# First two token tiles centred and turned through a diagonal of factors, head 0's q and k in alternating halves, head 4's q projected one slot earlier, in a four-block transformer kernel

## The chip, the cores and the metric

The kernel runs on one core of a Trainium2 chip. The time is the device time of one execution in microseconds. Three runs of the kernel before gave 628.95, 629.01 and 629.42 us, a median of 629.01 us. Engines are named as the profile names them: PE is the matrix engine (PEld its weight loads), DVE the vector engine, ACT the scalar engine, POOL the general-purpose engine, SP the engine that issues most DMAs.

## The reference, cut to what matters

Input `h` has 2 batches of 512 tokens and 256 features. Four blocks follow one another, each with a residual and layer norms around it; the change lies in the first block alone, softmax attention with 16 heads of 128:

```python
x = L0_attn_h
x = x + _layernorm(_L0_attn_ref(_layernorm(x), ...))          # 16 heads, softmax, rotary
x = x + _layernorm(_L0_ffn_ref(_layernorm(x), ...))           # 4-bit weights, gelu
x = x + _layernorm(_L1_attn_ref(_layernorm(x), ...))          # linear attention
x = x + _layernorm(_L1_ffn_ref(_layernorm(x), ...))           # looked-up weights, silu

def _L0_attn_ref(h, wq, bq, ...):
    x = (h - mu) * rsqrt(var + EPS) * ln_g + ln_b
    q = rope((x @ wq.T + bq).reshape(b, s, 16, 128))
    k = rope((x @ wk.T + bk).reshape(b, s, 16, 128))
    v = (x @ wv.T + bv).reshape(b, s, 16, 128)
    attn = softmax(where(causal, -inf, q k^T / sqrt(128)))
    return (attn @ v) @ wo.T + bo + h
```

The first block's input is normalised twice in a row (once outside, once inside), which the kernel folds into one factor per token.

## The kernel before, in words

Tokens are worked in tiles of 128 (`NT` = 4 tiles to a batch). All arithmetic is float32. Instructions are issued in the order in which the Python code runs, and each engine works through its own instructions in that order; across engines a tile's readers and writers wait for one another. Tiles come from pools of one or two buffers, and a buffer is written again when its last reader is done.

**The start.** `first_norms(0, 0.0)` (lines 554 to 688) normalises batch 0. For each tile DVE takes `statistics` (line 600) and `variance` (603); `factor` (606) adds the epsilons on DVE (`ve`) and raises to -0.5 on POOL (`rstd`). For tiles 0 and 1, `finished(t, pool)` (593) lets POOL form `shift = -mean * rstd` and ACT write `n = rstd * x + shift`. Tiles 2 and 3 are written by DVE in `centred` (609). PE transposes the eight 128x128 pieces of `n` (`turn`, 620) into two banks `halves`, ACT applies gain and bias (`affine`, 623) and so writes `xT0`, features on partitions and tokens along the free axis, in four pieces of 256 tokens. POOL and ACT copy it in another order to `xTv`. Before all that PE multiplies the identity by itself `WARM` = 9 times (line 538), and once more between tile 0 and tile 1 (line 662).

**The projections.** `projection(kind, i, tag)` (786) makes q or k of head `i` (heads of both batches are numbered 0 to 31): two matmuls, then the rotary turn. `a = (ps + bias) * cos` is one pass over 128x512, done by DVE, or by ACT with a POOL product behind it; `r` is two DVE passes over 64 partitions (`rr`), with `sin`; `a + r` is `qT` or `kT`. Head 0's q is done in two halves of 256 tokens, every other projection in one piece. `values` (826) makes v of two heads. Weights of two heads come in one load (`load`, 509) into one of two buffers per kind.

**The slots.** After q 0, k 0, the first v and q 1 (lines 1100 to 1103), `slot(i)` (998) runs once per head. In it PE does, in this order: scores of head `i` (6 matmul records in bank s, 2 in bank t), q of head `i+1`, k of head `i+1`, `projected_out(i-2)`, `attended(i-1)` (894), one `values`. q of head 3 is the exception: it is issued in slot 1 through the generator `ahead` (line 1078) ahead of `attended(0)`, and slot 2 leaves q out.

**The turned softmax.** `turned_p(i)` (876) has DVE transpose blocks of p into `turned` (one buffer), then SP issues four DMAs that bring it to `pT[i]`, a tile of a pool with one buffer (line 885). So the DMAs of head `i` start when `attended(i-1)`, the reader of the buffer, has ended; and the DVE transposes of head `i+1` wait until those DMAs have read `turned`.

Of the kernel before, what the change touches and what calls it, by code (L numbers as in the profile page):

```python
# [38 lines left out]
EPS = 1e-5  # L39
EPS_LIN = 1e-9  # L40
NEG = -1e30
WARM = 9
REST = INTER - (NO - 1) * P


# [143 lines left out]
def sandwich_kernel(  # L189
# [309 lines left out]
    with ExitStack() as at:  # L499
# [54 lines left out]
        def first_norms(b, wait):  # L554

            n = [
                acts.tile([P, HT, D], F32, tag="ln", name=f"n0_{b}_{j}") for j in range(NT // HT)  # L560
            ]
            st = small.tile([P, NT, 6], F32, tag="st0", name="st0", bufs=2)
            mv = small.tile([P, NT, 2], F32, tag="mv0", name="mv0", bufs=2)
            ve = small.tile([P, 2, NT], F32, tag="ve0", name="ve0", bufs=2)
            rstd = small.tile([P, 2, NT], F32, tag="rstd0", name="rstd0", bufs=2)
            shift = small.tile([P, 2, NT], F32, tag="shift0", name="shift0", bufs=2)

            def factors(k, ts, scale, more):
                vector.tensor_scalar(
                    ve[:, k, ts], mv[:, ts, 1], scale, more, ALU.mult, ALU.add  # L570
                )
                pool.tensor_tensor(rstd[:, k, ts], ve[:, k, ts], mhalf[:, ts], ALU.pow)

            def shifted(k, ts):
                vector.scalar_tensor_tensor(
                    shift[:, k, ts], mv[:, ts, 0], -1.0, rstd[:, k, ts], ALU.mult, ALU.mult
                )

            def shifted_row(t):
                pool.tensor_scalar(  # L580
                    shift[:, 0, t : t + 1], mv[:, t, 0:1], rstd[:, 0, t : t + 1], -1.0, ALU.mult, ALU.mult
                )

            def norm(k, t, to):
                scalar.activation(
                    to,
                    x0[b][:, t, :],
                    AF.Identity,
                    bias=shift[:, k, t : t + 1],
                    scale=rstd[:, k, t : t + 1],  # L590
                )

            def finished(t, engine=vector):
                if engine is pool:
                    shifted_row(t)
                else:
                    shifted(0, slice(t, t + 1))
                norm(0, t, n[t // HT][:, t % HT, :])

            def statistics(t):  # L600
                vector.bn_stats(st[:, t, :], x0[b][:, t, :])

            def variance(t):
                vector.bn_aggr(mv[:, t, :], st[:, t, :])

            def factor(t):
                factors(0, slice(t, t + 1), 1.0 + EPS, EPS * EPS)

            def centred(t):

                vector.tensor_scalar(
                    n[t // HT][:, t % HT, :],
                    x0[b][:, t, :],
                    mv[:, t, 0:1],
                    rstd[:, 0, t : t + 1],
                    ALU.subtract,
                    ALU.mult,
                )

            def turn(pt, kc, t):  # L620
                transpose(pt, n[t // HT][:, t % HT, kc * P : (kc + 1) * P])

            def affine(engine, to, pt, kc):
                if engine is scalar:
                    scalar.activation(to, pt, AF.Identity, bias=col("b", kc), scale=col("g", kc))
                else:
                    vector.tensor_scalar(to, pt, col("g", kc), col("b", kc), ALU.mult, ALU.add)

            if wait:
                for t in range(NT):  # L630
                    statistics(t)
                    variance(t)
                    factor(t)
                    if t:
                        finished(t - 1)
                    yield wait
                finished(NT - 1)
                yield 2 * wait
                for kc in range(NK):
                    pt = bank("t")  # L640
                    for t in range(NT):
                        turn(pt[:, t * P : (t + 1) * P], kc, t)
                    affine(scalar, xT0[b][:, kc, :], pt, kc)
                    yield wait
            else:


                for t in range(NT):
                    statistics(t)
                    variance(t)  # L650
                    factor(t)
                    if t < HT:
                        finished(t, pool)
                centred(2)
                centred(3)
                halves = [bank("t") for _ in range(2)]
                for t in range(NT):
                    for kc in range(NK):
                        at = kc * TU + t % 2 * P
                        turn(halves[t // 2][:, at : at + P], kc, t)  # L660
                    if t == 0:
                        warm_up(1)
                for j in range(2):
                    for kc in range(NK):
                        affine(
                            scalar,
                            xT0[b][:, kc, j * TU : (j + 1) * TU],
                            halves[j][:, kc * TU : (kc + 1) * TU],
                            kc,
                        )  # L670
            for kc in range(NK):
                (scalar.copy if kc or wait else pool.tensor_copy)(
                    xTv[b][:, kc, :].rearrange("p (t a j) -> p t j a", t=NT, j=4),
                    xT0[b][:, kc, :].rearrange("p (t j a) -> p t j a", t=NT, j=4),
                )
            yield 30.0
            while holder[0] is not None:
                yield 4.0
            holder[0] = b
            every = slice(0, NT)  # L680
            factors(1, every, 1.0, EPS)
            yield 2.0
            shifted(1, every)
            yield 2.0
            for t in range(NT):
                norm(1, t, acc[:, t, :])
                pool.tensor_add(acc[:, t, :], acc[:, t, :], bo_sb)
                yield 3.0

        first = first_norms(0, 0.0)  # L690
        begin(first, next(first))
        pool.affine_select(
            out=mask,
            in_=mask,
            compare_op=ALU.is_ge,
            fill=NEG,
            base=S - P,
            pattern=[[-1, S]],
            channel_multiplier=1,
        )  # L700

        def dequantised(packed, scales, u, name, w):

# [82 lines left out]
        def projection(kind, i, tag="mm"):  # L786
# [7 lines left out]
            to = qk.tile([P, S], F32, tag=f"T{kind}", name=f"{kind}T")  # L794
            lo, hi = slice(0, 64), slice(64, 128)

            for cs in [slice(0, TU), slice(TU, S)] if (kind, i) == ("q", 0) else [slice(0, S)]:
                ps = bank(tag)
                for kc in range(NK):
                    matmul(  # L800
                        ps[:, cs],
                        w[:, kc, hh * DK : (hh + 1) * DK],
                        xT0[b][:, kc, cs],
                        kc == 0,
                        kc == NK - 1,
                    )
                yield
                if (kind == "k") == (i > 1) and i:
                    scalar.activation(a, ps, AF.Identity, bias=bias)
                    pool.tensor_mul(a, a, cos_sb)  # L810
                else:
                    vector.scalar_tensor_tensor(
                        a[:, cs], ps[:, cs], bias, cos_sb[:, cs], ALU.add, ALU.mult
                    )
                vector.scalar_tensor_tensor(
                    r[lo, cs], ps[hi, cs], bias[hi], sin_sb[hi, cs], ALU.add, ALU.mult
                )
                vector.scalar_tensor_tensor(
                    r[hi, cs], ps[lo, cs], bias[lo], sin_sb[lo, cs], ALU.add, ALU.mult
                )  # L820
            if (kind, i) == ("k", 1):
                inverted(0)
            (pool if i > 1 or kind == "q" else vector).tensor_add(to, a, r)
# [174 lines left out]
        def slot(i):  # L998
            b, h = divmod(i, NH)
            g2, odd = divmod(i, HG)  # L1000
            if i == 2:
                load("q", 2)
                load("k", 2)
            if odd == 0:
                load("v", g2 + 2)
# [45 lines left out]
            else:  # L1051
                assert not terms
            for kind in "qk":
                if (kind, i) in (("q", 0), ("q", 2)):
                    pass
                elif i + 1 < NS:
                    project(kind, i + 1)
# [15 lines left out]
                values(0, 1, "t")  # L1073
            elif i == 1:
                values(1, 1, "t")
            if i == 1:

                ahead = projection("q", 3)
                next(ahead)
            if 1 <= i < NS + 1:  # L1080
                attended(i - 1)
# [1 line left out]
                values(1, 0)  # L1083
            if now_in:
                turned_p(i)
            if i == 1:
                next(ahead, None)
            poll()
            if i < NS - HG:
# [7 lines left out]
                look_up(done)  # L1097
            catch_up()

        project("q", 0)  # L1100
        project("k", 0, "o")
        values(0, 0, "t")
        project("q", 1, "o")

# [310 lines left out]
```

## Time and profile before

| | |
|---|---|
| median of three runs | 629.01 us |
| the profiled execution's own time | 629.14 us |
| span of its profile | 627.3 us |
| PE's first matmul on data (a transpose) | 5.66 us |
| first `xT` piece begun by ACT | 7.01 us |
| first score matmul of head 0 | 14.99 us |
| first score matmul of head 1 | 22.39 us |
| last matmul's end in the chain of waits | 619.76 us |
| granted clock of PE in every slice | 0.9 or more of full |

A line of a timeline gives start, duration (both in us), engine, line of the code, operation, what it writes and reads, its shape, how many records are merged, and in brackets the idle time of the engine before it with what ended it. A float32 matmul leaves two records. A group of PE records ends later than the next group starts[...]; so I compare starts with starts. Line 181 and line 163 are those of a helper that records each instruction, so instructions are told apart by the tiles they write and read.

### The profile page before, as it was taken

To read this page: it belongs to the slowest core of one execution; us is meant where nothing else is said; L and a number is where in the kernel's file an instruction comes from. 1 tells how busy PE (TensorE), PEld (TensorE's weight loads), DVE (VectorE), ACT (ScalarE), POOL (GpSimd) and SP (SyncE) were. 2 spreads that over 40 slices of the span, in tenths; PEclk is the share of its full clock that TensorE was granted. 3 is DMA by queue.
4 is the path that set the end of the run, shared out by engine and by line. 5 is a ranking of instruction groups with operands and counts; after the bars stand their busy time and mean duration, and the time that the engine had idled before them with its cause. 6 is when DMAs were issued, how large, how long until landed. Compare 5 with 4: busy or idle time off the path is not lost.

```text
span 627.3 us, 8200 instructions
## 1 busy us (share of the span) xinstructions
PE 619.3 (99%) x2504; PEld 461.7 (74%) x2504; DVE 486.5 (78%) x1154; ACT 298.1 (48%) x654; POOL 276.8 (44%) x350
## 2 busy tenths in 40 slices
PE   8999999999999999999999999999999999999996
PEld 6656666666666666666666778888888888888886
DVE  6969889878877989999988988769986373284853
ACT  4655666666655566656656661232313404416130
POOL 4354657446355375575667400350261151163341
PEclk9999999999999999999999999999999999999999
DMA  7376475464565656557453322211001001001000
GB/s 252 89 182 178 118 179 153 107 192 121 130 169 137 151 151 156 152 135 184 125 133 82 85 54 67 101 35 34 1 2 33 1 1 35 0 2 33 26 27 17
DMA packets 42428, 60.07 MB, mean 96 GB/s; under 512 B 5008, under 2 KB 29840, under 8 KB 42384
## 3 DMA queue, kind: packets, MB, share of 16 engines
q1 hardware_dynamic: 42096, 59.39, 36.3%
q8 instruction: 20, 0.33, 0.2%
q14 instruction: 24, 0.20, 0.1%
q10 hardware_dynamic: 288, 0.16, 0.1%
HBM read 28.33 MB, written 1.05 MB: 47 GB/s over the span
## 4 chain that ended last, share of the span: by engine, by line
PE 96%; DMA 1%; POOL 1%; issue 0%; DVE 0%; SPq 0%; POOLq 0%
PE ps_mm L272 39%; PE ps_o L272 22%; PE ps_s L272 21%; PE ps_t L272 14%; DMA pT<-turned 1%; POOL rstd L181 0%; DMA x<-in_x 0%; SPq L163 0%; PE ps_t L278 0%; DVE st L181 0%; POOL shift L181 0%; POOLq L1411 0%; DVE x L181 0%; DVE n L181 0%; DVE mv L181 0%
## 5 line engine op out<-in xcount | busy, mean ns | idle before, releaser
L181 POOL TENSOR_TENSOR wg<-wg,scratch 128x752 f32<-128x752 f32 x30 | 53.7, 1791 | 95.1 <-DVE scratch L181 95.1
L181 DVE SCALAR_TENSOR_TENSOR rr<-ps_mm,cols_sb,sin_sb 64x512 f32<-64x512 f32 (+1 forms) x126 | 93.4, 741 | 2.8 <-ACT ra L181 0.4
L272 PE MATMUL ps_mm<-xT,wg 128*128 128x256 f32 (+1 forms) x352 | 84.9, 379 | 0.0
L181 ACT ACTIVATE p<-p,mn 128x512 f32<-128x512 f32 (+3 forms) x128 | 70.6, 552 | 29.3 <-DVE mn L181 29.3
L272 PE MATMUL ps_s<-xT,wu 128*128 128x256 f32 x336 | 81.0, 379 | 0.0
L272 PE MATMUL ps_o<-wd,hT 128*128 128x256 f32 (+1 forms) x364 | 78.2, 372 | 0.0
L272 PE MATMUL ps_t<-pT,v 128*128 128x512 f32 (+3 forms) x256 | 74.3, 433 | 1.3 <-DMA pT<-turned 1.3
L272 PEld LDWEIGHTS ps_o<-wd,hT 128*128 128x128 f32 x364 | 67.4, 190 | 8.8
L272 PEld LDWEIGHTS ps_mm<-xT,wg 128*128 128x128 f32 (+1 forms) x352 | 66.4, 189 | 9.3 <-ACT ge L181 0.3
L272 PEld LDWEIGHTS ps_s<-xT,wu 128*128 128x128 f32 x336 | 63.8, 190 | 8.7
L272 PEld LDWEIGHTS ps_t<-pT,v 128*128 128x128 f32 x256 | 48.6, 190 | 29.2 <-issue 17.5
L181 DVE CUSTOM_DVE_ANT_0 p<-ps_s,mask 128x512 f32<-128x512 f32 (+2 forms) x96 | 45.9, 509 | 30.3 <-PE ps_s L272 30.1
L181 ACT ACTIVATE p<-p,rs 128x512 f32<-128x512 f32 (+3 forms) x128 | 61.4, 550 | 10.8 <-DVE rs L181 8.8
L272 PEld LDWEIGHTS ps_o<-wo,oT 128*128 128x128 f32 x256 | 48.6, 190 | 19.0 <-issue 13.2
L181 POOL TENSOR_TENSOR qT<-ra,rr 128x512 f32<-128x512 f32 x32 | 40.9, 1277 | 48.0 <-DVE rr L181 46.2
L272 PE MATMUL ps_s<-kT,qT 128*128 128x512 f32 (+2 forms) x192 | 60.8, 452 | 0.1
L272 PE MATMUL ps_o<-wo,oT 128*128 128x256 f32 x256 | 60.5, 379 | 0.0
L272 PE MATMUL ps_mm<-xT,wq 128*128 128x512 f32 (+1 forms) x128 | 58.4, 580 | 0.0
L272 PE MATMUL ps_mm<-xT,wk 128*128 128x512 f32 x124 | 58.3, 592 | 0.0
L181 DVE STREAM_TRANSPOSE turned<-p 128x512 f32<-128x512 f32 (+3 forms) x128 | 54.1, 480 | 2.1 <-DMA pT<-turned 1.0
L272 PEld LDWEIGHTS ps_s<-kT,qT 128*128 128x128 f32 x192 | 36.0, 190 | 26.8 <-issue 15.9
L272 PE MATMUL ps_mm<-wv,xTv 128*128 128x256 f32 x232 | 54.9, 379 | 0.0
(138 smaller groups left out, 910.6 us busy)
## 6 DMA issues: line engine op xcount, KB each, us to landing
pT<-turned SPq DMA_DIRECT2D x128, 208.0 KB, 3.8
wo<-in_wo SPq DMA_DIRECT2D x17, 256.0 KB, 4.2
wq<-in_wq SPq DMA_DIRECT2D x16, 256.0 KB, 4.0
wk<-in_wk SPq DMA_DIRECT2D x16, 256.0 KB, 4.1
wv<-in_wv SPq DMA_DIRECT2D x16, 256.0 KB, 4.1
xT<-tr SPq DMA_DIRECT2D x44, 64.0 KB, 2.1
pk_g<-in_gate_p SPq DMA_DIRECT2D x4, 256.0 KB, 4.9
sc_g<-in_gate_s SPq DMA_DIRECT2D x8, 128.0 KB, 4.6
```

The costliest lines, as they stand in the source:

```text
L181: return write(*args, **more)
L272: nc.tensor.matmul(out, lhsT=lhsT, rhs=rhs, start=start, stop=stop, **more)
```

## The change

Tiles 0 and 1: ACT writes `mean - x` as soon as the mean is known, without the factor. `rstd` of both tiles comes from one pair of two-element instructions. ACT builds, per tile, a diagonal matrix with `-rstd` (from `minus`, the negated identity; all three lie in the tile `wu`, which is not yet in use). Four ordinary matmuls with that diagonal as the moving operand then turn and scale `n` at once. Tiles 2 and 3 are still transposed with the identity; their four transposes stand after q 0's first half, since `first_norms` now yields in between.

Head 0: q and k both come in halves, in the order q first half, (transposes of tiles 2 and 3), k first half, q second half, k second half. In the first halves DVE does the two `rr` passes first, and the `a` pass goes to ACT and POOL (`by_scalar`). POOL's `affine_select` of the mask moves from before head 0 to behind it.

Head 4: its q is issued in slot 2 through `ahead`, in front of `attended(1)`; slot 3 leaves q out. Its weights (`load("q", 2)`) are loaded in slot 0 in place of slot 2. `WARM` goes from 9 to 10, and the single warm-up matmul between tiles goes.

```diff
-WARM = 9
+WARM = 10
...
-            def factor(t):
-                factors(0, slice(t, t + 1), 1.0 + EPS, EPS * EPS)
+            def factor(t, n=1):
+                factors(0, slice(t, t + n), 1.0 + EPS, EPS * EPS)
...
+                minus = wu[:, 0, :P]
+                scalar.mul(minus, ident, -1.0)
                 for t in range(NT):
                     statistics(t)
                     variance(t)
-                    factor(t)
                     if t < HT:
-                        finished(t, pool)
+                        scalar.activation(
+                            n[0][:, t, :], x0[b][:, t, :], AF.Identity, bias=mv[:, t, 0:1], scale=-1.0
+                        )
+                    if t % HT:
+                        factor(t - 1, HT)
+                halves = [bank("t") for _ in range(2)]
+                for t in range(HT):
+                    scalar.activation(
+                        wu[:, 0, (t + 1) * P : (t + 2) * P],
+                        minus,
+                        AF.Identity,
+                        scale=rstd[:, 0, t : t + 1],
+                    )
+                for kc in range(NK):
+                    for t in range(HT):
+                        matmul(
+                            halves[0][:, kc * TU + t * P : kc * TU + (t + 1) * P],
+                            n[0][:, t, kc * P : (kc + 1) * P],
+                            wu[:, 0, (t + 1) * P : (t + 2) * P],
+                            True,
+                            True,
+                        )
                 centred(2)
                 centred(3)
-                halves = [bank("t") for _ in range(2)]
-                for t in range(NT):
-                    for kc in range(NK):
-                        at = kc * TU + t % 2 * P
-                        turn(halves[t // 2][:, at : at + P], kc, t)
-                    if t == 0:
-                        warm_up(1)
                 for j in range(2):
+                    if j:
+                        yield 0.0
+                        for kc in range(NK):
+                            for t in (HT, HT + 1):
+                                at = kc * TU + t % 2 * P
+                                turn(halves[1][:, at : at + P], kc, t)
...
-            for cs in [slice(0, TU), slice(TU, S)] if (kind, i) == ("q", 0) else [slice(0, S)]:
+            for cs in [slice(0, TU), slice(TU, S)] if i == 0 else [slice(0, S)]:
...
-                if (kind == "k") == (i > 1) and i:
-                    scalar.activation(a, ps, AF.Identity, bias=bias)
-                    pool.tensor_mul(a, a, cos_sb)
-                else:
+                def by_scalar():
+                    scalar.activation(a[:, cs], ps[:, cs], AF.Identity, bias=bias)
+                    pool.tensor_mul(a[:, cs], a[:, cs], cos_sb[:, cs])
+
+
+                first_half = i == 0 and cs.start == 0
+                if i and (kind == "k") == (i > 1):
+                    by_scalar()
+                elif not first_half:
...
+                if first_half:
+                    by_scalar()
...
-            if i == 2:
+            if i == 0:
                 load("q", 2)
+            elif i == 2:
                 load("k", 2)
...
-                if (kind, i) in (("q", 0), ("q", 2)):
+                if kind == "q" and i in (0, 2, 3):
...
-            if i == 1:
-
-                ahead = projection("q", 3)
+            if i in (1, 2):
+
+                ahead = projection("q", i + 2)
                 next(ahead)
...
-            if i == 1:
+            if i in (1, 2):
                 next(ahead, None)
...
-        project("q", 0)
-        project("k", 0, "o")
+        pair = projection("q", 0), projection("k", 0, "o")
+        next(pair[0])
+        begin(first, next(first))
+        next(pair[1])
+        for step in (*pair, *pair):
+            next(step, None)
+        pool.affine_select(
...
         values(0, 0, "t")
         project("q", 1, "o")
```

More of the change, by code (lines that the diff above doesn't have):

```diff
@@ L577, in shifted @@
                 )
[L579 to L582, printed above, removed]
             def norm(k, t, to):
@@ L591, in norm, with finished @@
                 )
-            def finished(t, engine=vector):
-                if engine is pool:
-                    shifted_row(t)
-                else:
-                    shifted(0, slice(t, t + 1))
+            def finished(t):
+                shifted(0, slice(t, t + 1))
                 norm(0, t, n[t // HT][:, t % HT, :])
@@ L690, in sandwich_kernel @@
         first = first_norms(0, 0.0)
[L691 to L700, printed above, removed]
+        next(first)
         def dequantised(packed, scales, u, name, w):
@@ L807, in projection @@
                 yield
-                if (kind == "k") == (i > 1) and i:
-                    scalar.activation(a, ps, AF.Identity, bias=bias)
-                    pool.tensor_mul(a, a, cos_sb)
-                else:
+                def by_scalar():
[5 more added lines that the diff above has]
+                elif not first_half:
                     vector.scalar_tensor_tensor(
@@ L1098, in slot @@
             catch_up()
-        project("q", 0)
-        project("k", 0, "o")
+        pair = projection("q", 0), projection("k", 0, "o")
[5 more added lines that the diff above has]
+        pool.affine_select(
+            out=mask,
+            in_=mask,
+            compare_op=ALU.is_ge,
+            fill=NEG,
+            base=S - P,
+            pattern=[[-1, S]],
+            channel_multiplier=1,
+        )
         values(0, 0, "t")
```

## The prediction, made before the changed kernel ran

> **What bounds the kernel.** I read the page first: which engine is full, and what still ends its idle time. Then PE's timeline around the one wait that the page names, then the chain of waits across it, then the timeline of the start.
>
> ```profile
> span 627.3 us, 8200 instructions
> ...
> PE 619.3 (99%) x2504; PEld 461.7 (74%) x2504; DVE 486.5 (78%) x1154; ACT 298.1 (48%) x654; POOL 276.8 (44%) x350
> ...
> L272 PE MATMUL ps_t<-pT,v 128*128 128x512 f32 (+3 forms) x256 | 74.3, 433 | 1.3 <-DMA pT<-turned 1.3
> ```
>
> PE is busy 619.3 of 627.3 us. So an edit pays only if it shortens PE's work, or one of the few stretches in which PE stands: the start, one wait of 1.3 us on the DMA that brings pT, and the tail after the last matmul (619.76 us), which the change does not touch. PE's timeline shows the wait:
>
> ```profile
> 37.49 1.89 PE L272 MATMUL ps_o<-wo,oT 128*128 128x256 f32 x8
> 40.73 2.39 PE L272 MATMUL ps_t<-pT,v 128*128 128x512 f32 x8 [1.34 <-DMA pT<-turned]
> 42.96 1.89 PE L272 MATMUL ps_mm<-wv,xTv 128*128 128x256 f32 x8
> ...
> 52.00 2.32 PE L272 MATMUL ps_t<-pT,v 128*128 128x512 f32 x8
> 54.16 1.89 PE L272 MATMUL ps_mm<-wv,xTv 128*128 128x256 f32 x8
> ```
>
> An eight-record group starts 1.72 us after the one before it (50.28 to 52.00 in slot 3), so `attended(1)` could have started at 37.49 + 1.72 = 39.21; it started at 40.73, 1.52 late, and then took 2.23 (to 42.96) where slot 3's takes 2.16. The wait costs 1.52 + 0.07 = **1.6 us**. The chain of waits says why:
>
> ```profile
> 31.62 2.17 PE ps_t L272 x8
> 33.79 0.02 issue
> 33.81 0.54 SPq L163
> ...
> 35.95 4.64 DMA pT<-turned
> 40.59 0.14 issue
> 40.73 2.39 PE ps_t L272 x8
> ```
>
> pT has one buffer, so head 1's DMAs go out only when `attended(0)` has ended (33.79); issue and landing take to 40.59, and 0.14 later PE goes on: 40.73 - 33.79 = 6.94 us of turnaround. PE has too little to put in between: scores 2.16, k 1.72, out 1.72, in all 5.6.
>
> The start, as the timeline has it:
>
> ```profile
> 3.60 0.18 DVE L181 BATCH_NORM_AGGREGATE mv<-st 128x2 f32<-128x6 f32 x1
> 4.05 0.55 POOL L181 TENSOR_TENSOR rstd<-ve,mhalf 128x1 f32<-128x1 f32 x1 [2.25 <-DVE ve L181]
> 6.03 0.39 PE L536 MATMUL ps_o<-ident 128*128 128x128 f32 x2
> 6.54 1.28 PE L278 MATMUL ps_t<-ident,n 128*128 128x128 f32 x6
> 7.01 1.93 ACT L181 ACTIVATE xT<-ps_t,cols_sb 128x256 f32<-128x256 f32 x4 [0.53 <-PE ps_t L278]
> 7.65 2.05 PE L272 MATMUL ps_mm<-xT,wq 128*128 128x256 f32 x8
> 12.98 1.88 PE L272 MATMUL ps_o<-xT,wq 128*128 128x512 f32 x4
> 14.15 0.69 DVE L181 TENSOR_TENSOR kT<-ra,rr 128x512 f32<-128x512 f32 x1
> 14.99 1.96 PE L272 MATMUL ps_s<-kT,qT 128*128 128x512 f32 x6
> ```
>
> From 7.65 on PE is full, but for a short stall before the scores: q 1 starts at 12.98, so PE was free at 14.70; DVE's kT was done at 14.84 and the scores began at 14.99.
>
> **Part 1: q of head 4 into slot 2.** 1.72 us of PE work moves in front of `attended(1)`: 5.6 + 1.72 = 7.32 us against a turnaround of 6.94. The wait goes with 0.38 to spare: **-1.6 us**. What is late next is slot 3, which loses those 1.72. Between the end of `attended(1)` and `attended(2)` there are values 1.73, scores 2.16, k 1.72, out 1.72, again 7.33. Head 2's DMAs in the trace of before: `attended(1)` ends at 43.12 (40.73 + 2.39), the fourth is issued at 45.4 and lands after 4.3, 49.7, and with the same 0.14 PE could start 6.72 after the end. 0.6 to spare, cost nothing; slot 4's four needed 57.2 + 5.0 = 62.2, which is 7.9 after 54.32 (52.00 + 2.32), and such a landing in slot 3 would cost 8.0 - 7.33 = 0.7. I take the row of the same head, and keep 0.7.
>
> The other instructions of the moved step: DVE's `ra` and two `rr` (0.75 + 1.51 = 2.26) fall behind head 2's block transposes, which end at 42.41; DVE sits idle from there for 3.29 us until 45.75, so they are hidden, and slot 3's DVE is the freer by as much. POOL's qT sum (1.27) stands ahead of the four-element rstd of batch 0's second norm, which nothing waits for in that slot. In slot 3 POOL does the look-up sum (49.40 to 51.18, 6.5 after the slot's first score at 44.69), then k 4's product and sum, 2 x 1.27: kT at about 9.1 after that score, and the next scores come at 2.16 + 1.72 + 1.72 + 2.16 + 1.73 = 9.5. 0.2 to 0.4 to spare.
>
> The load of head 4's wq moves in SP's queue from slot 2 to slot 0, ahead of wv, wo and head 0's pT. It waits for q 1, the last reader of its buffer (about 15 us); wv behind it goes out at 20.86 because it waits for v's own readers, so nothing is held up. From 16 to 20 us the page's DMA row is near nothing, so it lands free. In slot 2 the loads behind head 1's pT are one fewer.
>
> **Part 2: the diagonal.** Removed: four POOL instructions for tiles 0 and 1 (two rstd, two shift) in series; added: one rstd of two elements, two diagonals, and matmuls for transposes. DVE: without the `ve` in between, tile 1's statistics start about 0.10 after 3.60, at 3.70 (before 3.88). Its aggregate is 0.45 later and `ve` 0.22 after that: 4.37. POOL starts 0.24 after `ve` as in the row: 4.61. One element takes 0.55, four take 1.03 (42.53 us), so two about 0.71: 5.32. ACT starts 0.04 later. Its two `mean - x` passes (0.60 each) and the negated identity are then done: they end by about 5.1. The diagonals: a 128x128 product by a column takes ACT 0.387, the second starts about 0.29 behind: ready at 5.75 and 6.04. PE follows 0.06 later; its second matmul starts at 6.10, two more at a spacing of 0.21, and the last takes 0.39, as the lone one at 6.03 did: 6.92, ACT begins xT at **6.95**, against 7.01.
>
> [...] The rows have transposes 0.11 apart, and 256-column float32 matmuls 0.43 apart (8.11 to 8.54), which is 0.21 for 128: a factor of 2. [...] I take the row, which is of this shape.
>
> [...] The row: the warm-up records stand 0.21 apart (half rate) up to 5.6, and at 6.03 a matmul's two stand 0.10 apart, so the clock came between 5.6 and 6.0. The ten warm-ups in a row end at about 1.38 + 20 x 0.21 + 0.2 = 5.8, so PE is not idle longer than before. If the clock came one matmul row too late, the last three double: +0.5.
>
> **Part 3: alternating halves.** PE after xT's start A = 6.95: first q matmul at A + 0.64 (7.65 - 7.01) = 7.59, second 0.46 behind (ACT's pace), 0.43; then four transposes 0.44 that before lay ahead of q, unseen; k half 0.86, q half 0.86, k half 0.86, v 1.72, q 1 1.72: scores at **14.94**. In the order of before these transposes cost nothing on this path, but q had three waits of 0.03 each and the scores 0.29 for kT. ACT's second xT pieces come at about A + 2.6 and 3.1, when PE is still in k's half: hidden. DVE: `rr` of q and k, then ra and rr of both second halves (0.48 + 0.98 each), then 0.69: kT at about 14.65, no longer last. sin lands at 3.52 + 5.0 = 8.5, and the first `rr` wants it at 8.8: just hidden. POOL, with xTv, two products of about 0.65 and 1.27 for qT, is done at about 14.4; the mask behind it takes 0.62, and DVE first needs it after 17 us.
>
> But q 1 ends 0.24 later than before (its start 13.22 against 12.98), and DVE's serial row behind it (rr of q 1, the score passes, ra and rr of k 1, kT) had only 0.18 of idle before kT 1 ended at 22.20 with the scores of head 1 at 22.39. So 0.24 - 0.18 = **+0.05** remains there. The start gains nothing; bounds: tile 1's data not there before 3.88 adds 0.18 to A, the late clock 0.5[...]; the other way, with A 0.15 earlier and kT no longer in the way, -0.3.
>
> **Sum.** -1.6 + 0.05 = -1.5 us. The profiled execution's 629.14 (span 627.3, 1.8 around it) becomes 627.6; the median shown lies 0.13 lower: **627.5**. About 0.2% (1.26 us) is what a measurement of this kernel tells from no change, so a result under 627.75 counts as faster.
>
> **Rivals.** *The wait moves to slot 3.* For it: slack of only 0.6 and slot 4's 7.9 us. Against: head 2's own row of 6.6. Price up to 0.7: 628.2; chance 0.10. *The start gets slower* by late data, late clock or slow diagonals, +0.5 to +0.6: 628.1; chance 0.15. For it: DVE has no slack into kT 1. *The start gains*, -0.3 in place of +0.05: 627.1; chance 0.09. *Slower than before:* the clock stays at half after the warm-ups[...]. Every us of PE work then costs 0.5. It wipes out 1.5 us if 3 us of PE work run at half rate, to about 10.5 us; to be 0.2% slower it needs some 5.6 us, to about 13, giving 630.3 or more. Against it: before had pauses of 0.3 to 0.5 at the same place and full clock. Chance 0.04.
>
> **Chances.** The forecast has 0.62 with its own range 627.2 to 627.8, of which 0.53 lie under 627.75; with the gaining start 0.62 for faster. 0.34 same, 0.04 slower. For 8 in 10: 626.9 to 628.3.
>
> **What would show it.** PE's wait on pT near 40 us gone, and none in slot 3; ACT's first xT near 6.95; scores of head 0 near 14.9 and of head 1 near 22.4; `attended(1)` starting about 7.3 after `attended(0)` ends. Wrong, if any matmul group past 45 us waits, or if the first xT is later than 7.3.

## The result, and the profile after

| | before | changed |
|---|---|---|
| median of 20 runs each | 629.01 us | 628.00 us |
| lowest to highest | 628.80 to 629.57 | 627.79 to 628.96 |
| ratio, with its 95% interval | | 0.9985 (0.9978 to 0.9992) |
| the profiled execution, its span | 629.14, 627.3 | 628.46, 626.7 |

The change makes the kernel 1.0 us faster, 0.15%. That is inside the stated range (626.9 to 628.3), 0.5 us short of the forecast of 627.5, outside the forecast's own narrower range (627.2 to 627.8), and less than the 0.2% that the prediction had set for telling a change from none; the interval of the ratio does lie wholly below 1. The profiled execution of the changed kernel is one of its slower ones (628.46).

Of the page of the changed kernel, the span, the busy times and the group that had waited for pT:

```profile
span 626.7 us, 8226 instructions
...
PE 619.5 (99%) x2512; PEld 463.3 (74%) x2512; DVE 486.5 (78%) x1153; ACT 299.5 (48%) x659; POOL 276.4 (44%) x348
...
L272 PE MATMUL ps_t<-pT,v 128*128 128x512 f32 (+3 forms) x256 | 74.2, 433 | 0.0
```

PE has 0.2 us more to do, its 256 matmuls on pT no longer wait at all (1.3 before), and the span is only 0.6 shorter, where the wait alone had cost 1.6. PE's timeline, at the places shown of before:

```profile
6.28 1.39 PE L272 MATMUL ps_t<-wu,n 128*128 128x128 f32 x8 [0.26 <-ACT wu L181]
8.32 1.15 PE L272 MATMUL ps_mm<-xT,wq 128*128 128x256 f32 x4 [0.66 <-ACT xT L181]
9.31 0.60 PE L278 MATMUL ps_t<-ident,n 128*128 128x128 f32 x4
9.75 1.03 PE L272 MATMUL ps_o<-xT,wk 128*128 128x256 f32 x4
10.62 1.11 PE L272 MATMUL ps_mm<-xT,wq 128*128 128x256 f32 x4
11.56 1.03 PE L272 MATMUL ps_o<-xT,wk 128*128 128x256 f32 x4
...
15.87 1.90 PE L272 MATMUL ps_s<-kT,qT 128*128 128x512 f32 x6
...
23.25 1.96 PE L272 MATMUL ps_s<-kT,qT 128*128 128x512 f32 x6
...
40.12 1.88 PE L272 MATMUL ps_mm<-xT,wq 128*128 128x512 f32 x4
41.84 2.32 PE L272 MATMUL ps_t<-pT,v 128*128 128x512 f32 x8
...
51.33 2.32 PE L272 MATMUL ps_t<-pT,v 128*128 128x512 f32 x8
```

Head 4's q (40.12) fills the hole in front of `attended(1)`, and slot 3's `attended(2)` (51.33) has no wait either. But q of head 0 begins at 8.32, where it had been 7.65; head 0's scores at 15.87 for 14.99; head 1's at 23.25 for 22.39. In this pair of executions the start is 0.86 us later at head 1's scores. From there to slot 4's scores (55.21, against 55.89 before) 1.54 us are won. Everything behind that has the same length in both: the profiled execution's time less the start of head 1's scores is 606.75 us before and 605.21 after, and 605.13 to 605.29 in all twelve kernels traced with head 4's part.

So the question is the start. Its chain of waits (start, duration, what the time was for) runs over tile 1 of the input:

```profile
1.17 2.94 DMA x<-in_x
4.12 0.02 issue
4.14 0.44 DVE st L181
...
5.07 0.73 POOL rstd L181
5.80 0.02 issue
5.82 0.41 ACT wu L181
6.24 0.04 issue
6.28 1.40 PE ps_t L272 x8
7.68 0.02 issue
7.71 0.57 ACT xT L181
```

Tile 1's data came at 4.12, and its statistics began at 4.14; the prediction had them at 3.70. From there to the first `xT` it is 7.71 - 4.14 = 3.57 us, where the prediction had 3.25 and the kernel before took 7.01 - 3.88 = 3.13.

### The profile page after: what moved, and what is told of

Read it like the earlier page. It is cut to its first block, busy times and chain, and to the rows that moved or that the text cites. A ratio compares the mean times of both kernels' runs of the same rounds, so it can differ in the third digit from the quotient of the medians.

```text
span 626.7 us, 8226 instructions
## 1 busy us (share of the span) xinstructions
PE 619.5 (99%) x2512; PEld 463.3 (74%) x2512; DVE 486.5 (78%) x1153; ACT 299.5 (48%) x659; POOL 276.4 (44%) x348
## 4 chain that ended last, share of the span: by engine, by line
PE 98%; DMA 0%; issue 0%; DVE 0%; POOL 0%; ACT 0%; POOLq 0%; SPq 0%
PE ps_mm L272 39%; PE ps_o L272 22%; PE ps_s L272 22%; PE ps_t L272 15%; DMA x<-in_x 0%; PE ps_t L278 0%; POOL rstd L181 0%; DVE st L181 0%; POOLq L1437 0%; ACT xT L181 0%; DVE x L181 0%; ACT wu L181 0%; DVE mv L181 0%; SPq L163 0%; POOL shift L181 0%
## 5 line engine op out<-in xcount | busy, mean ns | idle before, releaser
L272 PEld LDWEIGHTS ps_s<-kT,qT 128*128 128x128 f32 x192 | 36.0, 190 | 26.6 <-issue 15.7
```

The source lines that it names most:

```text
L272: nc.tensor.matmul(out, lhsT=lhsT, rhs=rhs, start=start, stop=stop, **more)
```

## The experiments

All were timed in five interleaved rounds with the kernel before on the same chip; its medians there were 628.95 to 629.04 us. The 628.00 of the whole change is that of the result above. The intervals of the ratios are some 0.0008 to each side, 0.5 us, and several differences below are smaller; so the readings rest on medians together with places in the traces. Each kernel's own trace gives:

| kernel | median us | tile 1's statistics | first xT | q begins | head 1's scores | statistics to xT | q to scores |
|---|---|---|---|---|---|---|---|
| before | 629.0 | 3.88 | 7.01 | 7.65 | 22.39 | 3.13 | 14.74 |
| the change | 628.00 | 4.14 | 7.71 | 8.32 | 23.25 | 3.57 | 14.93 |
| head 4 part alone | 627.52 | 3.76 | 6.89 | 7.53 | 22.26 | 3.13 | 14.73 |
| start alone | 629.50 | 3.83 | 7.23 | 7.85 | 22.78 | 3.40 | 14.93 |
| halves, old norm | 627.75 | 3.90 | 7.14 | 7.76 | 22.69 | 3.24 | 14.93 |
| diagonals, old order | 627.80 | 3.79 | 7.19 | 7.81 | 22.56 | 3.40 | 14.75 |

Of the 0.86 us in the pair of executions above, 0.26 are tile 1's later data, 0.44 the path from statistics to xT and 0.19 the row behind q; q follows xT 0.03 sooner.

My theory after the result was: head 4's part is worth what was forecast, and the new start gives about a third of it back. The rival: the start is neutral, and the gain of head 4's part itself was smaller.

**1. Head 4's part alone.** The kernel before with only these edits:

```diff
-            if i == 2:
-                load("q", 2)
+            if i == 0:
+                load("q", 2)
+            elif i == 2:
...
-                if (kind, i) in (("q", 0), ("q", 2)):
+                if kind == "q" and i in (0, 2, 3):
...
-            if i == 1:
-                ahead = projection("q", 3)
+            if i in (1, 2):
+                ahead = projection("q", i + 2)
...
-            if i == 1:
+            if i in (1, 2):
                 next(ahead, None)
```

> The kernel before with head 4's q in slot 2 and its weights loaded in slot 0, nothing else changed. My theory (this part is worth 1.6 us, and the new start gives 0.6 of it back): 627.4 us, 1.6 below before and 0.6 below the whole change; no wait on pT in slot 2 or 3; scores of head 1 at 22.4. Rival (the wait goes only because the later start leaves SP and the DMAs more air, so the part alone brings about 1.0): 628.0.

Measured 627.52 us, ratio 0.9976 (0.9968 to 0.9985), no wait on pT anywhere, head 1's scores at 22.26. Theory right. All 12 runs (627.40 to 627.77) lie below all 20 of the whole change (627.79 to 628.96): the head 4 part without the rest is the better kernel.

**2. The start alone.** The whole change with those edits undone.

> The whole change without its head 4 part: the new start alone. My theory: 629.6 us, 0.6 above before, the scores of head 1 at 23.0 to 23.3, and the 1.3 us wait on pT back. Rival (the start is neutral or better, and the rest of the expected gain was lost behind 25 us): 629.0 or less, scores of head 1 at 22.4.

Measured 629.50, ratio 1.001 (1.0002 to 1.0018): slower than before, by 0.5, as the theory said; head 1's scores come at 22.78 in its trace, earlier than the theory's 23.0 to 23.3. The wait is back in PE's timeline of this kernel:

```profile
37.93 1.89 PE L272 MATMUL ps_o<-wo,oT 128*128 128x256 f32 x8
40.93 2.40 PE L272 MATMUL ps_t<-pT,v 128*128 128x512 f32 x8 [1.11 <-DMA pT<-turned]
```

The two parts add up: -1.5 and +0.5 make the -1.0 of the change.

**3. Halves kept, normalisation of before.** To split the start in two, tiles 0 and 1 get their one-element factors, POOL's shift, their transposes and the nine warm-up matmuls plus one back:

```diff
-                minus = wu[:, 0, :P]
-                scalar.mul(minus, ident, -1.0)
...
+                    factor(t)
+                    if t < HT:
+                        pool.tensor_scalar(shift[:, 0, t : t + 1], ...)
+                        norm(0, t, n[0][:, t, :])
...
+                        turn(halves[0][...], kc, t)
```

> The whole change with tiles 0 and 1 normalised and transposed as before (one-element factors, shift on POOL, warm-up 9 and 1), the alternating halves kept. My theory (the diagonal is what is late: it waits for tile 1's data before any factor is made, and its matmuls meet the clock at half): first xT at 7.0, scores of head 0 at 15.1, of head 1 at 22.5, time 627.5. Rival (the alternating halves cost the start as well): first xT at 7.0 but scores of head 1 at 23 or later, time 628.0.

Measured 627.75, ratio 0.998 (0.9973 to 0.9988), between theory and rival: 0.25 under the change, 0.23 over the head 4 part alone. Both parts of the new start cost, and about the same.

**4. The other corner: the diagonals, in the old order of head 0** (all transposes ahead of q, k in one piece, DVE doing each pass).

> Head 4's part and the change's own diagonals (both factors taken together), with head 0 in the order of before. The whole change against the same with the old normalisation says that the diagonals cost 0.25. Theory (that price is paid in any order): 627.75, 0.25 over the head 4 part alone. Rival (in the old order the transposes of tiles 2 and 3 stand ahead of q and hide part of the later xT): 627.5 to 627.6.

Measured 627.80, ratio 0.9981 (0.9972 to 0.9989). So with head 4's part there are 627.52 (neither), 627.75 (halves), 627.80 (diagonals) and 628.00 (both): 0.23 and 0.28 alone, 0.48 together. The old order does not hide the diagonals' price.

The last two columns of the table say the same without medians. From q to head 1's scores every kernel of the table with the change's halves takes 14.93, those in the old order 14.73 to 14.75: 0.2 us. From tile 1's statistics to xT the diagonals take 3.40 (3.57 in the execution of the change, where PE's full clock was granted from 6.79 us), the old norm 3.13 (3.24 with the halves): 0.27 us. ACT's timeline has the end of that path, in head 4's part alone and in this kernel:

```profile
5.76 0.60 ACT L181 ACTIVATE n<-x,shift,rstd 128x256 f32<-128x256 f32 x1 [0.28 <-POOL shift L181]
6.89 1.93 ACT L181 ACTIVATE xT<-ps_t,cols_sb 128x256 f32<-128x256 f32 x4 [0.53 <-PE ps_t L278]
```

```profile
5.47 0.69 ACT L181 ACTIVATE wu<-wu,rstd 128x128 f32<-128x128 f32 x2 [0.50 <-POOL rstd L181]
7.19 1.93 ACT L181 ACTIVATE xT<-ps_t,cols_sb 128x256 f32<-128x256 f32 x4 [1.03 <-PE ps_t L272]
```

With tile 1's statistics at nearly the same time (3.76 and 3.79), ACT begins the first diagonal 0.29 sooner than it begins tile 1's `n`, and xT still comes 0.30 later.

**5. Tile 1 on another queue**, since its landing starts the chain:

```diff
-    scalar.dma_start(out=cols_sb, in_=cols)
     for t in range(NT):
-        (scalar if t == HT else sync).dma_start(
+        (scalar if t == 1 else sync).dma_start(
...
+    scalar.dma_start(out=cols_sb, in_=cols)
```

> The whole change with tile 1 of the input loaded by the ACT queue as its first DMA, ahead of the columns of biases, and tile 2 by SP. My theory (the factors of both tiles wait for tile 1's data, which landed at 4.1): tile 1's statistics begin at about 3.5 to 3.7 in place of 4.14, first xT 0.4 to 0.6 earlier (7.1 to 7.3), time 627.4 to 627.7. Rival (the data is not it: the 16 DMA engines are full and any order lands tile 1 by 4.1, or the clock and the ACT passes are what is late): statistics still at 4.1, or xT still at 7.7; time 628.0.

Measured 628.24, ratio 0.9989 (0.9982 to 0.9995). The theory fell: tile 0's statistics began at 3.34 in place of 2.93, tile 1's right behind at 3.90, and xT came at 7.53. Tile 1 gains 0.24 on the change's profile but nothing on the other traces with paired factors, that is with `rstd` of both tiles taken together (3.63 to 4.04), and tile 0 loses 0.4. The DMA engines were as full as the rival has them in the trace of the change, with a share of 1.03 from 2 to 3 us and of 1.08 from 3 to 4.1. The clock was late here too, granted in full from 6.72 us, and the path from the statistics to xT took 3.63.

**6. A factor and a diagonal per tile**, PE turning tile 0 whole first:

```diff
-                    if t % HT:
-                        factor(t - 1, HT)
+                    factor(t)
...
+                        scalar.activation(wu[:, 0, (t + 1) * P : (t + 2) * P], minus, AF.Identity,
+                            scale=rstd[:, 0, t : t + 1])
...
-                for kc in range(NK):
-                    for t in range(HT):
+                for t in range(HT):
+                    for kc in range(NK):
```

> The whole change, but each tile of the first two gets its own factor (one-element rows) and its own diagonal as soon as it has it, and PE turns tile 0 whole before tile 1. My theory (the diagonal is late because both tiles' factors are taken together and wait for tile 1's data, and tile 1's diagonal stands behind tile 0's): from tile 1's statistics to the first xT 2.6 to 2.8 us in place of 3.4 to 3.6, time 627.3. Rival (the ordinary matmuls at a half clock and the ACT passes are what is late, not the pairing): 3.3 or more, time 627.8 to 628.0.

Measured 627.88, the rival's time, ratio 0.9983 (0.9976 to 0.999); statistics to xT 3.01, neither the theory's 2.6 to 2.8 nor the rival's 3.3. Its trace shows why not less: tile 0's diagonal was ready at 4.87, but PE was in the ten warm-up matmuls until its first product at 5.81, just before tile 1's diagonal at 5.87.

**7. The same in the old order of head 0**, and with nine warm-up matmuls in place of ten.

> Head 4's part and the diagonals per tile, with head 0 in the order of before: all transposes ahead of q, k in one piece, DVE doing every pass on head 0. My theory: first xT as in the per-tile run with the halves, but all of head 0's k behind it stays DVE-bound (kT 0.15 to 0.3 later than PE), so time 627.2, 0.2 to 0.3 under the head 4 part alone (627.52). Rival (an earlier xT is not used, because sin, cos or the DVE row behind q 1 is what is late): 627.5, no gain over the head 4 part alone.

Measured 627.50, ratio 0.9976 (0.9967 to 0.9986): the rival. PE's first product started at 5.19, and xT came at 6.45, 2.70 after the statistics and 0.44 before the head 4 part alone. But q still began at 7.58 (there 7.53), because the transposes of tile 3 stand in front of q, and tile 3 was ready at 7.25. Against the same order with paired factors and ten warm-ups (627.80) it gains 0.3; against no diagonals at all, nothing.

**8. The transposes of tiles 2 and 3 back in front of q**, in the whole change:

```diff
+                for t in (HT, HT + 1):
+                    for kc in range(NK):
+                        at = kc * TU + t % 2 * P
+                        turn(halves[1][:, at : at + P], kc, t)
                 for j in range(2):
                     if j:
                         yield 0.0
-                        for kc in range(NK):
-                            for t in (HT, HT + 1):
-                                at = kc * TU + t % 2 * P
-                                turn(halves[1][:, at : at + P], kc, t)
```

> The whole change, with the four transposes of tiles 2 and 3 back in front of q's first half. My theory (the halves cost the start because these transposes, which ran while PE waited for xT, now stand in PE's full row): PE's 0.66 us of idle time before q shrinks to about 0.2, scores of head 0 at first xT plus 7.7 to 7.8 in place of 8.16, time 627.7. Rival (DVE's row of passes decides, not PE's): scores of head 0 earlier but head 1's at first xT plus 15.5 as before, time 628.0.

Measured 628.02, ratio 0.9984 (0.9977 to 0.9992): the time is the rival's. PE did lose its idle time before q, but then waited for kT, in this kernel's timelines of PE and DVE:

```profile
7.03 0.76 PE L278 MATMUL ps_t<-ident,n 128*128 128x128 f32 x4
7.65 1.16 PE L272 MATMUL ps_mm<-xT,wq 128*128 128x256 f32 x4
...
15.30 1.96 PE L272 MATMUL ps_s<-kT,qT 128*128 128x512 f32 x6 [0.47 <-DVE kT L181]
```

```profile
9.13 0.98 DVE L181 SCALAR_TENSOR_TENSOR rr<-ps_mm,cols_sb,sin_sb 64x256 f32<-64x256 f32 x2 [1.83 <-DMA sin_sb<-in_sin]
```

DVE's first pass is now one with sin, which landed at 3.55 + 5.5 = 9.05 there; from it DVE has its row of passes to do without a break. Before, with q at the same 7.65, DVE's first pass began at 8.82, so about 0.3 us of DVE's delay is sin's in this execution. So the theory is not settled: in number 11 below, with the transposes in front and no wait for sin, it is 14.77 us from q to head 1's scores, nearly the 14.74 of the old order. The kernel of number 8 with sin loaded first was not run.

**9. Both of these together.**

> The per-tile factors and the transposes in front together, on the whole change. If both causes are right and add up: 627.0. If the second is covered once the first is gone (tiles 2 and 3 then come after xT): 627.3.

Measured 627.86, ratio 0.998 (0.9971 to 0.999). They don't add up to either number. Its profiled execution, at 627.39 its fastest, does come near the second: q begins at 7.59, behind the transposes of tile 3, whose `n` was ready at 7.26. Why the median lies 0.5 above it is open; what spreads such times follows below.

**10 to 12. sin loaded ahead of cos**, in the whole change, in number 9 and in number 6, since sin had shown up as a wait:

```diff
-        sync.dma_start(out=cos_sb, in_=cos)
         sync.dma_start(out=sin_sb, in_=sin)
+        sync.dma_start(out=cos_sb, in_=cos)
```

> The whole change with sin loaded ahead of cos. In the changed order DVE's first pass on head 0 is one with sin, the later of the two loads (in one trace it landed at 9.05 and DVE waited for it). Theory (sin's landing is what spreads and delays the changed start): 627.6 and a narrower spread. Rival (in the change as it stands xT comes so late that DVE's first pass, at 9.5, is behind any landing of sin): 628.0, unchanged.

> Per-tile factors, the transposes in front, and sin ahead of cos. With xT earlier DVE's first pass comes at 8.7, about when sin lands (8.0 to 9.05 in the traces so far). Theory: the 627.86 of the same kernel with cos first falls to 627.5, its best profiled execution (627.39) becoming the usual one. Rival (the spread comes from the input tiles and the clock): 627.8.

> Per-tile factors with the halves in the order of the change, and sin ahead of cos. Theory: from 627.88 to 627.6 (q's first half at 7.1 to 7.6, DVE's first pass at 8.2 to 8.7 without a wait). Rival: 627.9.

Measured 627.96 (0.9979 to 0.9992 about 0.9986), 627.76 (0.9972 to 0.9987 about 0.998) and 627.69 (0.9972 to 0.9986 about 0.9979). In the change as it stands sin is no cause: its first DVE pass comes at 9.52 with cos first, and at 9.27 with sin first it waits for PE, not for sin. In the other two the medians move by 0.1 and 0.2, less than these rounds can tell. None is better than the head 4 part alone.

What spreads the times of the changed start was seen on the way. Number 10's 21 runs fall in two groups, 13 at 627.89 to 627.98 and 8 at 628.20 to 628.72. Its profiled execution (628.20, of the upper group) has tile 1's statistics at 4.04, where the start alone had them at 3.83, and the eight records of its diagonals take 1.24 us, about the 1.23 of the diagonals-alone kernel, where the full clock was granted from 4.46: there the data was late. Another profile points to PE's clock. The eight records of the diagonals' matmuls, with what stands around them, in number 9 and in its sin-first twin number 11:

```profile
5.72 1.06 PE L272 MATMUL ps_t<-wu,n 128*128 128x128 f32 x8
```

```profile
5.81 1.73 PE L272 MATMUL ps_t<-wu,n 128*128 128x128 f32 x8
...
8.20 1.16 PE L272 MATMUL ps_mm<-xT,wq 128*128 128x256 f32 x4 [0.22 <-ACT xT L181]
```

In the first the records stand 0.11 apart, in the second 0.21 until about 7.1, and there q began at 8.20 in place of 7.59, in executions of 627.39 and 628.10 us. The traces record the full clock as granted from 5.62 us in the first and from 7.23 in the second. That late data and a late clock make the slow runs is read from single profiles; no run forced either.

## Why the prediction was right, and what it mis-sized

*Head 4's q in slot 2: -1.6.* Right. The head 4 part alone measures 627.52, 1.5 below its kernel of before; 1.54 us are won between head 1's and head 4's scores in the traces. Slot 3 has no wait, as head 2's own row had said. The room was smaller than written, though: the sum counted 7.32 from start to start, and `attended(0)` (32.36 + 2.32 = 34.68) ends 0.16 after the next group has started. So `attended(1)`, at 41.84, starts 7.16 after that end, and the slack over the turnaround of 6.94 was 0.22 in place of 0.38; in slot 3 it is 7.17 (44.16 to 51.33) in place of 7.33. The DMAs that the prediction read off the page as near idle from 16 to 20 us are so in the trace of before (a share of 0.00), but the page's slices, 15.7 us long, cannot show it. The moved load and the moved DVE passes cost nothing that can be seen.

*The start: +0.05.* This term failed. It measures +0.48 (628.00 against 627.52, and 629.50 against 629.02). The prediction's own sign of being wrong, a first xT later than 7.3, is met in the change's trace (7.71), where the data came at 4.12 and the full clock at 6.79, and not in the table's other two kernels with diagonals (7.19 and 7.23). By its steps:

- *xT at 6.95, 0.06 earlier than before.* The prediction took 0.18 of that from tile 1's statistics starting at 3.70, right behind tile 0's, and named the data as a bound only. The data decides: in the five traces with paired factors and the usual loading of the input the statistics began at 3.63 to 4.14 (mean 3.89), in the three of the table with the old norm at 3.76 to 3.90. So nothing is won there, and what counts is the path from there. That path was put at 3.25 and measures 3.40; the old one takes 3.13. ACT's first diagonal does begin sooner after `ve` than the old `n` did (1.01 against 1.33 us), but two diagonals and four matmuls follow: in the diagonals-alone kernel 5.47 to 7.19, 1.72 us, against 5.88 to 7.01, 1.13 us, before. From the second diagonal to xT, with the matmuls between, the sum had 0.91 and it takes 1.03. Together +0.27 where the sum had -0.06.
- *Alternating halves.* From q to head 1's scores the sum had 22.44 - 7.59 = 14.85; it is 14.93, against 14.74. That it came so near is partly luck, for two misses nearly cancel. From q to q 1 it takes 5.83 (8.32 to 14.15) where the sum had 5.63: q's halves take 0.99 and 0.94 (8.32 to 9.31, 10.62 to 11.56) for 0.89 and 0.86, and ACT's second pieces of xT, called hidden and begun at 9.95, are the likely reason for the second. From q 1 to head 1's scores it takes 9.10 where the sum had 9.22. The rest held: the transposes that had been free now stand in PE's row, and the stall for kT that they push away (0.29) is worth less than they cost (0.44).
- *The matmuls of the diagonals.* The sum had them 0.21 apart, from the row of the 256-column matmuls (1.72 us for four, 18.94 to 20.66 before). At the full clock they start 0.22 apart, with two records each (7.06 and 7.28 in the change), and four transposes of one record each take 0.44 (9.31 to 9.75), 0.11 apart: a factor of 2, so the row was right.
- *The clock.* Named as a possible 0.5; in the profiled execution, where the full clock was granted from 6.79 us, I put it at about 0.17 (3.57, for 3.40 in the two kernels where it was granted from 4.24 and 4.46).

The rival "the start gets slower, +0.5 to +0.6" is what happened, at 0.15 chance, and by its reasons only in part: a longer path through the diagonals (0.27) was among them, the price of the halves (0.2) was not. The result lies in the stated range because that range allowed for this rival; two thirds of part 1's gain came through.

## What to carry to other kernels

An edit that shortens a chain at its head buys nothing where the next link waits for a load; measure both versions from the moment the data is there. Work that PE did while it waited is free only there: moved behind the first real matmul it stands in the full row. Here 0.44 us of it cost 0.2, since a wait for another engine went at the same time, and moved back alone it won nothing, since that wait came back. Where a change bundles several edits, run each alone: here one edit carried all of the gain and the other two took a third of it back.

## What the runs showed of the hardware that was not expected

PE's full clock came at very different moments after the same first matmul at 1.38 us. The traces record it as granted from 4.24 us in the start-alone kernel, 4.46 in the diagonals-alone one, 5.90 before, 6.79 in the change and 7.23 in number 11 (the page's clock row counts the time before that as full). In the last four of these the spacing of the matmul records agrees: it goes from 0.21 to 0.11 us around these moments. The first nine warm-up matmuls are the same in all of these kernels. These are single executions of different kernels, and the moments spread over 3.0 us. In the 14 traces the full clock lasts 617.8 us in ten and 621.2 in four, 3.4 apart. What sets the moment or the length no run here shows.
